# A graph attention layer on one core: softmax tiles turned by DMA instead of by TensorE, score stacks written from PSUM by halves

## The chip, the cores and the metric

The kernel runs on one core of one Trainium2 chip. The metric is device time in microseconds, the median of several executions; lower is better. A core has TensorE (PE, with its weight loads listed as PEld), VectorE (DVE), ScalarE (ACT), GpSimd (POOL), and 16 DMA engines, which are fed mainly from the queue of SyncE (SP). Each engine takes its instructions in the order in which they were written, and waits on semaphores for what other engines make.

## The reference

A layer norm and a relu give h (384 nodes, 1024 features). Three projections of h, and a second projection of each, give q2, k2 and v2 in 16 heads of 64. A mask is built from 6528 edges. Then comes a masked softmax per head, its product with v2, an output projection, and the residual.

```
h = jnp.maximum(_layernorm(x, axis=-1), 0.0)
q = x @ wq.T + bq ; k = x @ wk.T + bk ; v = x @ wv.T + bv          # x here is h
q2 = (q @ wiq.T + biq).reshape(N, H, D).transpose(1, 0, 2)          # k2, v2 alike
scores = jnp.einsum('hnd,hmd->hnm', q2, k2) * scale + mask[None]
attn = jax.nn.softmax(scores, axis=-1)
out = jnp.einsum('hnm,hmd->hnd', attn, v2)
return x + (out.transpose(1, 0, 2).reshape(N, OUT_F) @ wo.T + bo)
```

All is float32 to nearly full precision.

## The kernel before

**Arithmetic.** Each float32 operand is split into a high part (float32r, made by ScalarE in `split_hi`, L71) and a low part, the difference (`split_lo`, L83, on VectorE or GpSimd, at L86). A product is three matmuls: high x high, high x low, low x high (`mm3`, L373). The weights come in chunks of 128 rows (0.5 MB): 8 each for v, q, iv and k, then iq and ik in turn (one pair of chunks makes q2 and k2 of two heads), then 8 for the output. A chunk is loaded five chunks ahead of its use, into four raw buffers, and split two chunks ahead.

**Stages.** From 0 to about 150 us: layer norm, the projections, and beside them the building of the mask by indirect DMA from GpSimd. From about 150 to 285 us: attention. It is a loop over steps (L825), one softmax tile a step; a tile is 128 nodes of one head against all 384, so a head is three tiles, t = 0, 1, 2, and there are 48 tiles.

**A step.** Step i writes, in this order, each to the engine that does it:
- TensorE: half of the step's fill, the score matmuls of tile i (`do_S`), the other half of the fill. The fill is q2/k2 chunks (`fill_qk`), later blocks of the output projection (`fill_o`); about eight matmuls a step.
- VectorE: `do_ttr` of tile i-1 (masked scores and their row minimum, from PSUM into an SBUF tile e); for t = 0 `do_low` of tile i-4.
- ScalarE: `do_exp` of tile i-2 with the row sums.
- VectorE: `do_norm` of tile i-3, the reciprocal of the row sums. For t = 1 and 2 GpSimd then multiplies e by it (L738). For t = 0 ScalarE writes the high plane in fp16 instead (`do_high`), and a step later VectorE the low plane (`do_low`, L748).
- Every third step TensorE turns tiles t = 1 and 2 of a head by three 128x128 transposes each into PSUM (`turn_mm`, L758), alternating with the six matmuls of an earlier head's product with v2 (`av_mm`, L773). ScalarE and VectorE copy the turned tiles to fp16 high and low parts (`do_pt`, L766 and L767). Tile t = 0 is turned by a DMA from SP (`do_turn`, L752).
- ScalarE and VectorE finish a head's product (`do_ao`), and every second head ScalarE and GpSimd split it (`do_aos`).
- Tasks: where a q2/k2 chunk begins, `qk_head` evacuates the chunk before it (`qk_done`), splits the weights two chunks on, and loads the one five on.

**Score stacks.** `qk_done` evacuates a chunk (128 rows, two heads of 64) into a tile nat, high on ScalarE (L384), low on VectorE (L385), and then copies pieces of it by DMA: four for q2, four for k2, so that one head's high and low parts lie above each other in the 128 partitions. The score is then two matmuls: stacked q (high over low) by k high over k high, and by k low over k low.

**Weight splits in the attention stage.** The low parts of the odd chunks are on GpSimd, those of the even ones on VectorE (`PAR`). The output weights are split at the steps in `WSTEPS`, with the low part on GpSimd for 2, 3, 4 and 6 (`OPOOL`).

**Output.** `fill_o` builds six blocks (three node tiles by two halves) over the eight chunks, in two parts of four chunks, with three PSUM banks "g". The sum of a finished first part (`ysum`, L663) frees its bank; `flush_y` writes it.

Of the kernel before, what the change touches and what calls it, by code (L numbers as in the profile page):

```python
# [26 lines left out]
def gnn_kernel(ctx: ExitStack, tc: tile.TileContext, x, edges, erows, etw, wq, wk, wv, wiq, wik, wiv, wo,  # L27
# [355 lines left out]
    def evac(ps, hi, lo, bias):  # L383
        nc.scalar.activation(hi, ps[:, :N], AF.Identity, bias=bias)  # L384
        nc.vector.scalar_tensor_tensor(lo, ps[:, :N], bias, hi.bitcast(F32), op0=OP.add, op1=OP.subtract)  # L385

# [6 lines left out]
    w = 0  # L393
# [125 lines left out]
    def v2_early():  # L519
        t = work.tile([128, 2, N], F32R, tag="nat", name="tv", bufs=2)  # L520
        tv = t.bitcast(F32).rearrange("p a n -> p (a n)")[:, :512]
        nc.scalar.activation(tv, accs[5], AF.Copy)
        accs[5] = tv
# [45 lines left out]
    gps = {}  # L569

    def qk_done(w):
        n, p = chunks[w]
        q2 = nc.scalar if p == 0 else nc.sync
        nat = work.tile([128, 2, N], F32R, tag="nat", name="nat", bufs=2)
        evac(gps[w], nat[:, 0, :], nat[:, 1, :], bc[:, (3 if n == "iq" else 4) * 8 + p:(3 if n == "iq" else 4) * 8 + p + 1])
        nf = nat.bitcast(F32)
        if n == "iq":
            qs = work.tile([128, 2, N], F32R, tag="qs", name="qs")
            qf = qs.bitcast(F32)
            nc.sync.dma_start(qf[0:64, 0, :], nf[0:64, 0, :])  # L580
            q2.dma_start(qf[64:128, 0, :], nf[0:64, 1, :])
            nc.sync.dma_start(qf[0:64, 1, :], nf[64:128, 1, :])
            q2.dma_start(qf[64:128, 1, :], nf[64:128, 0, :])
            stacks["q", p] = qs
        else:
            ks = work.tile([128, 2, 2, N], F32R, tag="ks", name="ks")
            kf = ks.bitcast(F32)
            for o in range(2):
                for r in range(2):
                    (q2 if r else nc.sync).dma_start(kf[r * 64:(r + 1) * 64, o, :, :], nf[o * 64:(o + 1) * 64, :, :])  # L590
            stacks["k", p] = ks
# [7 lines left out]
    def qk_head(w):  # L599
# [5 lines left out]
        split_lo(w + 2, nc.gpsimd if (w + 2) % 2 == PAR else None)  # L605
# [24 lines left out]
    DT = (0,)  # L630
    PRE, RATE, RATE_O, RATE_E = 84, 7.9, 8, 8
    WSTEPS = (37, 40, 42, 44, 47, 51)
    PAR, OPOOL, ODVE = 1, (2, 3, 4, 6), (2,)
# [38 lines left out]
    def fill_o():  # L672


        first = [(0, 0), (0, 1), (1, 0), (1, 1), (2, 0), (2, 1)]
        first += [(a, k) for k in (2, 3) for a in range(3)] + [(a, k) for a in range(3, 6) for k in range(KH)]
        for a, k in first:
            while now[0] < wready[k] or now[0] < 6 * k + OREADY:
                yield 0
            if k == 0:  # L680
                flush_y(1)
# [6 lines left out]
        todo = [(a, k) for k in range(KH, 7) for a in range(5)]  # L688
        while todo:
# [6 lines left out]
            if k == KH:  # L696
                flush_y(1)
# [7 lines left out]
    def do_S(i):  # L705
# [4 lines left out]
        for s in range(2):  # L710
            nc.tensor.matmul(ps[:, :N], qs[:, o, t * 128:(t + 1) * 128], ks[:, o, s, :], start=(s == 0), stop=(s == 1))  # L711

    def do_ttr(i):
        t = i % 3
        e = es[i] = work.tile([128, N], F32, tag="e", name="e", bufs=EB)
        s = sts[i] = work.tile([128, 4], F32, tag="s", name="s", bufs=12)
        nc.vector.tensor_tensor_reduce(e, st_ps.pop(i)[:, :N], ma[:, t, :], -0.125, 3.0e38, OP.add, OP.min, s[:, 0:1])  # L717

    def do_exp(i):
        s = sts[i]  # L720
        nc.scalar.activation(es[i], es[i], AF.Exp, bias=s[:, 0:1], scale=-1.0, accum_out=s[:, 1:2])  # L721
# [3 lines left out]
    def pt_setup():  # L725
# [4 lines left out]
        plv.extend(f[:, 2 * j:2 * j + 2, :] for j in range(3))  # L730

    def do_norm(i):
        s = sts[i]
        nc.vector.reciprocal(s[:, 2:3], s[:, 1:2])  # L734
        if i % 3 in DT:
            nc.vector.tensor_scalar(s[:, 2:3], s[:, 2:3], PSC, None, op0=OP.mult)
        else:
            nc.gpsimd.tensor_tensor(es[i], es[i], s[:, 2:3].to_broadcast([128, N]), OP.mult)  # L738

    planes = {}  # L740

# [172 lines left out]
```

## Time and profile before

| | |
|---|---|
| median of 3 runs | 294.54 us (294.42 to 294.67) |
| profiled execution | 294.56 us, its span 292.8 us |
| TensorE clock granted | 1.0 throughout |
| attention stage | about 150 to 285 us |
| score matmuls of the first and the last tile | 160.1 and 265.1 us |
| DMA moved | 54.6 MB, 187 GB/s over the span |

A line of a group names the kernel line, engine, operation, output and inputs, shape and count, then the busy time and the mean of one. In a timeline the first two columns are the start and the duration in us; a wait ahead of an instruction, with what ended it, stands in brackets. Matmuls are pipelined, so that one starts before the one ahead of it has ended; the cost of one is the distance between starts. PEld is the row of weight loads; its share shows best how dense TensorE's work is.

### The profile page before, as it was taken

The numbers are of one execution on the slowest core, as the hardware profiler recorded it, in microseconds if no ns is written. First come the engines' busy times: TensorE is split into PE (matmuls) and PEld (weight loads), VectorE is DVE, ScalarE is ACT, GpSimd is POOL, SyncE is SP. The second block draws the span as 40 slices with busy tenths as digits, with TensorE's granted clock in tenths as the row PEclk, the third lists the DMA queues.
The fourth block names the chain that finished last, engine by engine and source line by source line (L and its number), as shares of the span: only waits on it lengthen the run. The fifth ranks groups of instructions, "written<-read, shape, count | busy, mean of one in ns | idle before, by whom it ended". The sixth has DMA issues, their size and how long they took to land. (4 is left out here: it accounts for less than half of the span.)

```text
span 292.8 us, 4859 instructions
## 1 busy us (share of the span) xinstructions
PE 284.7 (97%) x1610; PEld 267.4 (91%) x1610; DVE 208.2 (71%) x509; ACT 159.7 (55%) x291; POOL 154.8 (53%) x153
## 2 busy tenths in 40 slices
PE   6999999999999999999999999999999999989995
PEld 5999999999988889999999999999999998868874
DVE  3858996667665452999966768878786876788623
ACT  3894543244331222343643778787878788766510
POOL 3765576437775787992004256262627268636210
PEclk9999999999999999999999999999999999999999
DMA  7799857973463342278438879879797969901105
GB/s 268 248 321 404 292 209 254 323 242 112 143 189 122 121 146 72 72 224 296 154 86 227 241 208 211 212 166 227 166 234 147 254 133 234 230 2 27 27 3 215
DMA packets 33305, 54.60 MB, mean 187 GB/s; under 512 B 17408, under 2 KB 20992, under 8 KB 33280
## 3 DMA queue, kind: packets, MB, share of 16 engines
q1 hardware_dynamic: 30896, 51.90, 61.4%
q0 software_dynamic: 2064, 1.80, 2.2%
q10 hardware_dynamic: 320, 0.59, 0.8%
q8 instruction: 13, 0.21, 0.3%
q14 instruction: 12, 0.10, 0.1%
HBM read 38.30 MB, written 3.39 MB: 142 GB/s over the span
## 5 line engine op out<-in xcount | busy, mean ns | idle before, releaser
L374 PE MATMUL g<-g,whl 128*128 128x384 f32 x312 | 105.8, 339 | 0.0
L376 PE MATMUL g<-g,whl 128*128 128x384 f32 x312 | 104.3, 334 | 0.0
L375 PE MATMUL g<-g,whl 128*128 128x384 f32 x312 | 104.2, 334 | 0.0
L231 POOL DMA_INDIRECT tab<-val,idx x51 | 59.7, 1171 | 32.0 <-issue 11.8
L81 ACT ACTIVATE whl<-raw 128x1024 fp32r<-128x1024 f32 x51 | 53.5, 1050 | 29.8 <-PE g L376 21.1
L86 DVE TENSOR_TENSOR whl<-raw,whl 128x1024 fp32r<-128x1024 f32 x41 | 53.8, 1313 | 20.1 <-ACT whl L81 17.0
L374 PEld LDWEIGHTS g<-g,whl 128*128 128x128 f32 x312 | 58.6, 188 | 0.2
L375 PEld LDWEIGHTS g<-g,whl 128*128 128x128 f32 x312 | 58.6, 188 | 0.0
L376 PEld LDWEIGHTS g<-g,whl 128*128 128x128 f32 x312 | 58.6, 188 | 0.1
L390 ACT ACTIVATE g<-f,bc 128x384 fp32r<-128x384 f32 x24 | 14.8, 618 | 53.7 <-DVE f L389 44.8
L738 POOL TENSOR_TENSOR e<-e,s 128x384 f32<-128x384 f32 x32 | 26.4, 829 | 31.2 <-DVE s L734 23.0
L86 POOL TENSOR_TENSOR whl<-raw,whl 128x1024 fp32r<-128x1024 f32 x11 | 26.3, 2395 | 25.9 <-ACT whl L81 25.0
L721 ACT ACTIVATE e<-e,s 128x384 f32<-128x384 f32 x48 | 29.1, 607 | 2.0 <-DVE s L717 1.2
L717 DVE CUSTOM_DVE_ANT_0 e<-s,ma 128x384 f32<-128x384 f32 x48 | 26.4, 552 | 4.3 <-PE s L711 3.7
L389 DVE TENSOR_TENSOR f<-g,rrow 128x384 f32<-128x384 f32 x24 | 13.3, 554 | 18.0 <-PE g L376 18.0
L773 PE MATMUL a<-pt,vhl 128*128 128x384 f16 x96 | 26.1, 326 | 0.0
L758 PE MATMUL t<-ident,e 128*128 128x128 f32 x96 | 24.9, 272 | 0.0
L711 PE MATMUL s<-ks,qs 128*128 128x384 f32 x96 | 24.5, 335 | 0.0
L767 DVE SCALAR_TENSOR_TENSOR pt<-t,pt 128x384 f16<-128x384 f32 x32 | 16.6, 549 | 8.2 <-ACT pt L766 8.2
L799 POOL TENSOR_TENSOR g<-aof,g 128x384 fp32r<-128x384 f32 x8 | 8.3, 1041 | 25.5 <-ACT g L798 25.5
L711 PEld LDWEIGHTS s<-ks,qs 128*128 128x128 f32 x96 | 17.5, 188 | 0.9
L744 ACT ACTIVATE pt<-e,s 128x384 f16<-128x384 f32 x16 | 9.9, 616 | 15.4 <-issue 9.4
(166 smaller groups left out, 447.0 us busy)
## 6 DMA issues: line engine op xcount, KB each, us to landing
ks<-nat SPq DMA_DIRECT2D x30, 192.0 KB
raw<-in_wv_dram SPq DMA_DIRECT2D x8, 512.0 KB
raw<-in_wq_dram SPq DMA_DIRECT2D x8, 512.0 KB
raw<-in_wiv_dram SPq DMA_DIRECT2D x8, 512.0 KB
raw<-in_wk_dram SPq DMA_DIRECT2D x8, 512.0 KB
raw<-in_wiq_dram SPq DMA_DIRECT2D x8, 512.0 KB
raw<-in_wik_dram SPq DMA_DIRECT2D x8, 512.0 KB
raw<-in_wo_dram SPq DMA_DIRECT2D x8, 512.0 KB
```

The costliest lines, as they stand in the source:

```text
L81: nc.scalar.activation(dst[0], raw[w], AF.Copy)
L86: (eng or nc.vector).tensor_tensor(lo, raw[w], hi.bitcast(F32), OP.subtract)
L231: nc.gpsimd.indirect_dma_start(out=tabs[c // RNG], out_offset=bass.IndirectOffsetOnAxis(ap=idx[:, c:c + 1], axis=0), in_=val[:, c:c + 1], ...
L374: nc.tensor.matmul(ps, lhi, rhi, start=first, stop=False)
L375: nc.tensor.matmul(ps, lhi, rlo, start=False, stop=False)
L376: nc.tensor.matmul(ps, llo, rhi, start=False, stop=last)
L711: nc.tensor.matmul(ps[:, :N], qs[:, o, t * 128:(t + 1) * 128], ks[:, o, s, :], start=(s == 0), stop=(s == 1))
L717: nc.vector.tensor_tensor_reduce(e, st_ps.pop(i)[:, :N], ma[:, t, :], -0.125, 3.0e38, OP.add, OP.min, s[:, 0:1])
L721: nc.scalar.activation(es[i], es[i], AF.Exp, bias=s[:, 0:1], scale=-1.0, accum_out=s[:, 1:2])
L738: nc.gpsimd.tensor_tensor(es[i], es[i], s[:, 2:3].to_broadcast([128, N]), OP.mult)
L758: nc.tensor.transpose(ps[:, k * 128:(k + 1) * 128], es[i][:, k * 128:(k + 1) * 128], ident)
L773: nc.tensor.matmul(ps[:, :N], vhl[:, k, h, :, :], ptv[h % 3][:, 3 * s + k, :], start=(k == 0 and s == 0), stop=(k == 2 and s == 1))
```

## The change

- **Turning.** `DT` becomes (0, 1, 2): all three tiles of a head are turned by DMA, except tiles 1 and 2 of the last head. So 46 tiles of 48 go by DMA and two by TensorE; before, 16 and 32.
- **Planes.** Every tile turned by DMA gets a high and a low plane. The high plane is ScalarE's for t = 0 and GpSimd's for t = 1 and 2 (`PHI`), where it takes the place of the multiplication by the reciprocal; the low plane is VectorE's for all. One reciprocal of three columns, after the head's last tile, serves all three. The planes are made two steps later than before (`LAG`), in five buffers instead of three.
- **Order.** A head's product with v2 comes one step later (3h + 11), but for the last head.
- **Score stacks.** The evacuation writes the stacks directly, by halves of 64 partitions: high to its place, low across to the other half. For k2, a second copy of the high part goes by DMA, two copies a pair; the stacks of k2 lie in two fixed buffers whose other low half is set to zero once.
- **Weight splits.** All low parts in this stage that `qk_head` issues go to GpSimd.
- **Output.** The blocks of the first part come block by block for two chunks at a time; the sums are written at the end of each step; two steps of `WSTEPS` move (37 to 36, 40 to 38).

```
-    def evac(ps, hi, lo, bias):
-        nc.scalar.activation(hi, ps[:, :N], AF.Identity, bias=bias)
-        nc.vector.scalar_tensor_tensor(lo, ps[:, :N], bias, hi.bitcast(F32), op0=OP.add, op1=OP.subtract)
...
+    ksb = []
+    for j in range(2):
+        ksb.append(work.tile([128, 2, 2, N], F32R, tag="ks", name="ks"))
+        for o in range(2):
+            nc.gpsimd.memset(ksb[j].bitcast(F32)[64 - o * 64:128 - o * 64, 1, o, :], 0.0)
...
+        for o in range(2):
+            m, l = slice(o * 64, o * 64 + 64), slice(64 - o * 64, 128 - o * 64)
+            hi, lo = (qs[m, o, :], qs[l, o, :]) if n == "iq" else (ks[m, 0, o, :], ks[m, 1, o, :])
+            nc.scalar.activation(hi, ps[m, :N], AF.Identity, bias=bias[m])
+            if n == "ik":
+                kf = ks.bitcast(F32)
+                (nc.scalar if p == 0 and o else nc.sync).dma_start(kf[l, 0, o, :], kf[m, 0, o, :])
+            nc.vector.scalar_tensor_tensor(lo, ps[m, :N], bias[m], hi.bitcast(F32), op0=OP.add, op1=OP.subtract)
...
-        split_lo(w + 2, nc.gpsimd if (w + 2) % 2 == PAR else None)
+        split_lo(w + 2, nc.gpsimd)
...
-    DT = (0,)
+    DT, LAG, PHI = (0, 1, 2), 2, (1, 2)
-    WSTEPS = (37, 40, 42, 44, 47, 51)
-    PAR, OPOOL, ODVE = 1, (2, 3, 4, 6), (2,)
+    WSTEPS = (36, 38, 42, 44, 47, 51)
+    OPOOL, ODVE = (2, 3, 4, 6), (2,)
...
-        first = [(0, 0), (0, 1), (1, 0), (1, 1), (2, 0), (2, 1)]
-        first += [(a, k) for k in (2, 3) for a in range(3)] + [(a, k) for a in range(3, 6) for k in range(KH)]
+        first = [(a, k) for c in (0, 2) for a in range(3) for k in (c, c + 1)]
+        first += [(a, k) for a in range(3, 6) for k in range(KH)]
...
-        todo = [(a, k) for k in range(KH, 7) for a in range(5)]
+        todo = [(a, k) for k in range(KH, 7) for a in (0, 1, 3, 4, 2)]
...
+    def by_dma(i):
+        return i % 3 in (DT if i < S - 3 else (0,))
...
+        last = max(c for c in range(3) if by_dma(3 * h + c))
+        if by_dma(i) and t < last:
+            return
+        c = slice(0, t + 1) if by_dma(i) else slice(t, t + 1)
+        nc.vector.reciprocal(s[:, 2, c], s[:, 1, c])
...
+        planes[i] = plv[next(npl) % len(plv)]
+        if i % 3 in PHI:
+            nc.gpsimd.tensor_tensor(planes[i][:, 0, :], es[i], factor(i).to_broadcast([128, N]), OP.mult)
+        else:
+            nc.scalar.activation(planes[i][:, 0, :], es[i], AF.Copy, scale=factor(i))
...
-        a_at[3 * h + 10 if h < 15 else 3 * h + 9] = h
+            if not by_dma(3 * h + t):
+                t_at.setdefault(3 * h + 7 if h < 15 else 3 * h + 5 + t, []).append(3 * h + t)
+        a_at[3 * h + 11 if h < 15 else 3 * h + 9] = h
...
-        if 0 <= i - 4 < S and (i - 4) % 3 in DT:
+        if 0 <= i - 4 - LAG < S - 3 and by_dma(i - 4 - LAG):
+            do_low(i - 4 - LAG)
+        if i - 4 == S - 3:
             do_low(i - 4)
...
+        for j in [i - 3 - LAG] if i - 3 - LAG < S - 3 else []:
+            if j >= 0 and by_dma(j):
+                do_high(j)
...
+        flush_y()
```

## The prediction

> **What bounds the kernel now.** I read the page's shares first, then a table by stage, then TensorE's instructions in order, then groups by tile, then VectorE and GpSimd side by side.
>
> From the page, and from the table by stage (columns: stretch, its length, busy PE, PEld, DVE, ACT, POOL, clock, DMA share, GB/s):
> ```profile
> PE 284.7 (97%) x1610; PEld 267.4 (91%) x1610; DVE 208.2 (71%) x509; ACT 159.7 (55%) x291; POOL 154.8 (53%) x153
> ...
> 170.00:240.00 70.00, 70.00 (x430) 68.06 (x430) 53.89 (x159) 56.36 (x126) 34.12 (x31) 1.00 0.85 194
> ```
> TensorE has no gap in the attention stage: 70 of 70 us, weight loads 97%. VectorE has 77%, ScalarE 81%, GpSimd 49%. TensorE's order sets the pace.
>
> TensorE in order of time, then a piece of the chain that ended last:
> ```profile
> 200.14 0.27 PE L758 MATMUL t<-ident,e 128*128 128x128 f32 x1
> 200.25 0.33 PE L773 MATMUL a<-pt,vhl 128*128 128x384 f16 x1
> 200.41 0.27 PE L758 MATMUL t<-ident,e 128*128 128x128 f32 x1
> ...
> 260.25 0.50 PE L374 MATMUL g<-whl,g 128*128 128x512 f32 x1 [1.37 <-DVE res L663]
> ```
> ```profile
> 279.27 0.99 PE a L773 x6
> ```
> A busy time overlaps the next one; starts give the price. Turn and product together take 0.27 us; six products alone take 0.99, 0.165 each. So a turn costs TensorE 0.107, not the 0.272 of its row. The last line of the first fence is the stage's one stall, 1.4 us for a bank that an output sum holds.
>
> The group by tile of the planes (min/median/max), and VectorE and GpSimd in order of time:
> ```profile
> L748 DVE SCALAR_TENSOR_TENSOR pt<-e,s,pt x16: 611/619/1754, 166.6 to 267.9; 128x384 f16<-128x384 f32 x16
> L752 SPq DMA_TRANSPOSE pt<-pt x16: 1212/1234/1825, 172.5 to 269.7; - x16
> ```
> ```profile
> 219.74 0.56 ACT L384 ACTIVATE nat<-g,bc 128x384 fp32r<-128x384 f32 x1
> 220.21 1.05 ACT L81 ACTIVATE whl<-raw 128x1024 fp32r<-128x1024 f32 x1
> 220.31 0.83 POOL L738 TENSOR_TENSOR e<-e,s 128x384 f32<-128x384 f32 x1
> 220.34 0.62 DVE L385 SCALAR_TENSOR_TENSOR nat<-g,bc,nat 128x384 fp32r<-128x384 f32 x1 [0.79 <-ACT nat L384]
> 220.87 0.55 DVE L717 CUSTOM_DVE_ANT_0 e<-s,ma 128x384 f32<-128x384 f32 x1
> 221.33 2.39 POOL L86 TENSOR_TENSOR whl<-raw,whl 128x1024 fp32r<-128x1024 f32 x1 [0.20 <-ACT whl L81]
> 221.34 0.16 DVE L734 RECIPROCAL s<-s 128x1 f32<-128x1 f32 x1
> ...
> 266.82 2.40 POOL L86 TENSOR_TENSOR g<-raw,g 128x1024 fp32r<-128x1024 f32 x1 [2.08 <-ACT g L81]
> 267.88 1.75 DVE L748 SCALAR_TENSOR_TENSOR pt<-e,s,pt 128x384 f16<-128x384 f32 x1 [0.24 <-ACT pt L744]
> ```
> The reader is to see the one long low plane. It began 1.06 us into a GpSimd subtraction, waited for its end at 269.22 and ended 0.41 us later: 1.13 us lost. The evacuation at 220.34, with PSUM as one source, ran 0.62 us beside GpSimd and lost nothing. The splits at 121.57 and 130.06, which read two SBUF tiles on VectorE, took 2.43 and 2.37 us instead of 1.23 beside GpSimd's residual sum.
>
> **What leaves TensorE.** 30 tiles x 3 turns x 0.107 = 9.6 us. A head takes 6.86 us now (the groups of products end at 180.29 and, nine heads on, 242.07); without six turns 6.22. Output sums at the end of each step, and the new order of blocks, put the sum of the first block two steps ahead of its bank's next use: the 1.4 us stall goes (bounds 0 and 1.5).
>
> **What the other engines gain, a head.** A start-to-start cost is below the duration; I take 0.50 for the mask-and-minimum, 0.53 for a low plane, the head's sum and a half evacuation.
> - VectorE: 5.29 (53.89 over 10.2 heads), less two low parts from PSUM (0.549 each), two reciprocals (0.156; for the joint one the 128x3 row of 0.17) and half a weight split (1.226), plus two low planes (0.62) and a second half evacuation (0.62): about 5.1.
> - ScalarE: 5.5 less two copies (0.482) plus one half evacuation (0.574; by the 64-partition row 0.669): 5.1.
> - GpSimd: 3.3 plus half a split (2.39): 4.5. The high planes replace the norms at 0.829; fp16 output has no GpSimd row, so bounds 0.83 and the 1.04 of the ao split; I take 0.83, the same form.
> - SP: three transposes (1.23, worst 1.83), a load and one copy (about 0.6 each): 4.9 of 6.22.
> - DMA: a transpose kept the 16 engines busy for about 1.0 us (271.0 to 272.0, 197 KB). Two more a head add 2 us; the pair's copies fall from 1.18 MB to 0.2 MB, which at that rate takes away 2.5 a head. Neutral.
> - The four memsets of the zero halves (0.41 each by the 128x384 row) lie at 140 to 150 us, where GpSimd is idle.
> - One step more before a head's product costs TensorE nothing while the turns land. A transpose lands 2.2 us after its issue begins (269.71 to 271.9); with a 0.5 MB load (1.5, at the 350 GB/s of the fastest half microseconds) and a copy ahead about 4.5, of three steps, 6.2. Bounds 0 and 1 us a head; I take 0.
>
> All fits under 6.22 by load. What doesn't fit is the order.
>
> **The wait that is added.** A low plane reads two SBUF tiles; there are now three a head, one in every step, and every weight split is on GpSimd, where 2.39 us is longer than any pause between low planes. Follow a step that opens a chunk of q2/k2 (steps 1, 4, ..., 34). On ScalarE: half, half, split high. On VectorE behind them: half, half, mask-and-minimum, low plane. In the fence above that race stands without the second half, which delays both alike: from the evacuation's start GpSimd's subtraction began after 1.59 us, and VectorE's instruction in the low plane's place after 1.60. The subtraction also had to be first only just: at 130.06 GpSimd had started 0.02 us before VectorE and VectorE waited it out. Where it loses, the low plane waits 2.4 us; behind it stand the head's reciprocals, behind those ScalarE's high plane of tile 0, and behind that, in ScalarE's order, the next chunk's evacuation and split. That closes a loop:
> - subtraction 2.39; low plane's rest, reciprocal and factor to ScalarE 0.75 (0.41 after the subtraction; 224.34 to 224.76, less the 0.08 by which the reciprocal starts early);
> - ScalarE: high 0.52, exp 0.60, head's bias 0.69, exp 0.60, ao 0.41 every second head, two halves 0.47 each;
> - split high 1.05 and the hop 0.07.
>
> Sum 7.8 us a head, over TensorE's 6.22 and over the 6.86 of now. Where the low plane wins, the head runs at 6.22, but tile 0's plane then meets what is left of the subtraction (about 1.2 us), VectorE falls behind and the next race is lost by over 0.6: two heads in 14.0, 7.0 each. With two races in three lost I take 7.4. Ten splits (steps 7 to 34) meet low planes: 10 x (7.4 - 6.22) = 11.8 us. GpSimd's four output-weight splits (steps 36, 38, 42, 47) meet low planes too, but VectorE has no evacuations then (1.06 a head): 0 to 1 us each; 1.5 in all.
>
> [...]
>
> [...]
>
> **Sum.** The profiled execution took 294.56 (span 292.8), the median is 294.54: no correction. 294.56 - 9.6 - 1.4 + 11.8 + 1.5 = 296.9, say 297. Its own range: all heads at 7.0 and no later cost, 291; all at 7.8 and 4 later, 303.
>
> **The rivals.**
> - *TensorE stays the bound* (the other side). Place: the low plane behind a chunk's evacuation. The subtraction falls into time that VectorE and ScalarE have to spare (18% by load) and no loop forms. For it: loads of 5.1, 5.1 and 4.5 against 6.22, and 15 of 16 low planes undisturbed today. Against it: today one step in three has a low plane, and it stands ahead of the split. 294.56 - 11.0 + 1.5 = 285. It decides at a delay of (294.56 - 285)/10 = 0.96 us a head: below it the change is faster.
> - *The transposes are late.* SP or the 16 DMA engines hold each head's product up. For it: SP at 79%, issues of up to 1.83 us when the DMA is full (share 0.85 now). Against: DMA load unchanged, some 1.7 us of slack. At 1.2 us for 14 heads: 283.6 + 16.8 = 300; it decides at 0.79.
> - *The turns cost nothing on TensorE*, hidden beside products. Excluded by the starts above.
>
> **How the numbers follow.** Loop 0.52 (slower 0.45, same 0.03, faster 0.04: its low end lies just under the time of now); TensorE bound or a little above it, 283 to 291, 0.38, all faster; late transposes 0.08, slower; the rest, 0.02, no change. Faster 0.42, same 0.05, slower 0.53 (0.2%, 0.6 us, is about what a measurement here can tell). The range 285 to 303 leaves out some 0.12 below, the better end of the bound TensorE, and 0.07 above.
>
> **What would show it.** Right: low planes with a median near 0.6 and every third or so over 1.5 us, ending 0.4 after a GpSimd subtraction; ScalarE's high plane waiting for VectorE's factor; heads 7 to 7.8 us apart; weight loads well under 97%; TensorE waiting for VectorE in the score tiles. Wrong: heads 6.2 to 6.4 apart and weight loads still at 97% (first rival), or TensorE waiting for DMA at the head's product (second). The forecast falls if GpSimd's subtraction regularly starts after the low plane, or if the low plane's wait lies in VectorE's spare time.

## The result, and the profile after

The changed kernel takes 331.88 us (median of 4 runs, 330.38 to 332.09), the kernel before beside it 294.61 (294.42 to 295.71). The ratio is 1.1246, with a 95% interval of 1.1203 to 1.1288: 37 us slower. The profiled execution took 332.09, its span is 330.4.

The page of the kernel after, and its table by stage (columns as before: stretch, length, busy PE, PEld, DVE, ACT, POOL, clock, DMA share, GB/s):

```profile
PE 290.1 (88%) x1520; PEld 256.8 (78%) x1520; DVE 234.5 (71%) x487; ACT 159.6 (48%) x277; POOL 181.5 (55%) x165
```
```profile
170.00:270.00 100.00, 73.10 (x365) 60.40 (x363) 78.83 (x146) 57.07 (x118) 51.35 (x36) 0.97 0.55 121
...
180.00:190.00 10.00, 7.74 (x33) 6.62 (x33) 6.25 (x11) 3.90 (x10) 4.07 (x3) 0.83 0.90 184
```

TensorE was busy 70 of 70 us before (170 to 240 us) and is now busy 73 of 100 (170 to 270 us). No engine has taken its place: VectorE, the busiest, has 79%, and part of that is waiting inside its instructions: its 30 low planes in this stretch take 22.5 us more than at 0.61 us each, its 11 scalings of the factors 2.0 more than at 0.17. What is lost is lost in waits. The view of waits between 150 and 330 us (who waited, for whom, us in total, times, longest) names three engines in a ring:

```profile
PE s L704 <- DVE s L712: 30.0, 30, 2.2
ACT pt L757 <- DVE s L745: 20.0, 8, 2.7
...
ACT pl L757 <- DVE s L745: 15.2, 6, 3.4
...
ACT ks L582 <- DVE ks L586: 9.2, 8, 3.6
ACT qs L582 <- PE s L704: 8.5, 6, 2.8
```

ScalarE waits 35.2 us for the joint factor of a head's three tiles (L745). TensorE waits 30 us for VectorE to free a score bank (L712). ScalarE also waits for VectorE between the halves of a chunk (L586 before the second L582). Here is one head, from one GpSimd subtraction (L86) to the next, in order of time:

```profile
209.50 2.39 POOL L86 TENSOR_TENSOR whl<-raw,whl 128x1024 fp32r<-128x1024 f32 x1 [2.29 <-ACT whl L81]
...
209.51 2.79 DVE L761 SCALAR_TENSOR_TENSOR pt<-e,s,pt 128x384 f16<-128x384 f32 x1
...
212.23 0.17 DVE L743 RECIPROCAL s<-s 128x3 f32<-128x3 f32 x1
212.43 0.17 DVE L745 TENSOR_SCALAR s<-s 128x3 f32<-128x3 f32 x1
...
212.63 0.61 ACT L757 ACTIVATE pt<-e,s 128x384 f16<-128x384 f32 x1 [2.61 <-DVE s L745]
...
213.15 0.60 ACT L717 ACTIVATE e<-e,s 128x384 f32<-128x384 f32 x1
...
213.87 0.67 ACT L806 ACTIVATE aot<-a,bc,vsc 64x384 f32<-64x384 f32 x1
...
214.57 0.61 ACT L717 ACTIVATE e<-e,s 128x384 f32<-128x384 f32 x1
...
215.31 0.58 ACT L582 ACTIVATE ks<-g,bc 64x384 fp32r<-64x384 f32 x1
...
216.12 0.60 DVE L586 SCALAR_TENSOR_TENSOR ks<-g,bc,ks 64x384 fp32r<-64x384 f32 x1
...
216.76 0.58 ACT L582 ACTIVATE ks<-g,bc 64x384 fp32r<-64x384 f32 x1 [0.88 <-DVE ks L586]
...
217.36 1.06 ACT L81 ACTIVATE whl<-raw 128x1024 fp32r<-128x1024 f32 x1
...
218.49 2.39 POOL L86 TENSOR_TENSOR whl<-raw,whl 128x1024 fp32r<-128x1024 f32 x1 [3.83 <-ACT whl L81]
```

GpSimd started 0.01 us ahead of the low plane, and the low plane (L761) took 2.79 us instead of 0.61: it ended only after the subtraction had. Such a wait of a VectorE instruction for a GpSimd one, or the other way round, inside its own time, is called a wait at the port below; the word is a name only, since the traces show the wait and not what the two engines share. Behind the low plane stand the reciprocal and the factor, behind the factor ScalarE's high plane (it had waited 2.61), and behind that, in ScalarE's order, exponential, bias, exponential, two halves and the next weight split, which starts the next subtraction. Such low planes of 2.77 to 2.84 us start at 179.78, 190.50, 199.53 and so on to 266.46, ten in ten heads. A head that closes with a k2 chunk takes 8.99 us (209.50 to 218.49), one with a q2 chunk 9.98 (199.52 to 209.50); before it was 6.86.

From the score matmul of tile 0 to that of tile 36, before takes 77.4 us (160.28 to 237.63) and after 106.2 (160.42 to 266.60), 28.8 more. From tile 36 to 47, it is 27.5 and 33.7, 6.2 more. That is 35.0 of the 37.3 us.

### The profile page after: what moved, and what is told of

Read it like the earlier page. It is cut to its first block, busy times and chain, and to the rows that moved or that the text cites. A ratio compares the mean times of both kernels' runs of the same rounds, so it can differ in the third digit from the quotient of the medians.

```text
span 330.4 us, 4621 instructions
## 1 busy us (share of the span) xinstructions
PE 290.1 (88%) x1520; PEld 256.8 (78%) x1520; DVE 234.5 (71%) x487; ACT 159.6 (48%) x277; POOL 181.5 (55%) x165
## 4 chain that ended last, share of the span: by engine, by line
PE 54%; DVE 25%; ACT 8%; issue 7%; POOL 2%; DMA 2%; SPq 0%; DVEq 0%; ACTq 0%; POOLq 0%
PE g L376 13%; PE g L374 13%; PE g L375 13%; DVE pt L761 7%; DVE e L712 6%; DVE pl L761 4%; DVE qs L586 2%; ACT aot L806 2%; ACT qs L582 2%; DMA g<-in_x_dram 2%; DVE ks L586 2%; PE s L704 2%; ACT e L717 2%; PE s L374 2%; PE s L376 2%
## 5 line engine op out<-in xcount | busy, mean ns | idle before, releaser
L374 PE MATMUL g<-g,whl 128*128 128x384 f32 x312 | 107.0, 343 | 0.0
L376 PE MATMUL g<-g,whl 128*128 128x384 f32 x312 | 105.6, 338 | 0.0
L375 PE MATMUL g<-g,whl 128*128 128x384 f32 x312 | 105.5, 338 | 0.0
L86 POOL TENSOR_TENSOR whl<-raw,whl 128x1024 fp32r<-128x1024 f32 x19 | 47.4, 2497 | 62.7 <-ACT whl L81 54.7
L704 PE MATMUL s<-ks,qs 128*128 128x384 f32 x96 | 28.8, 382 | 32.8 <-DVE s L712 30.0
L86 DVE TENSOR_TENSOR whl<-raw,whl 128x1024 fp32r<-128x1024 f32 x33 | 44.1, 1336 | 15.3 <-ACT whl L81 15.3
L761 DVE SCALAR_TENSOR_TENSOR pt<-e,s,pt 128x384 f16<-128x384 f32 x28 | 35.0, 1249 | 2.8 <-ACT pt L757 1.6
L712 DVE CUSTOM_DVE_ANT_0 e<-s,ma 128x384 f32<-128x384 f32 x48 | 26.4, 552 | 2.6 <-PE s L704 1.5
L761 DVE SCALAR_TENSOR_TENSOR pl<-e,s,pl 128x384 f16<-128x384 f32 x18 | 20.5, 1141 | 2.7 <-POOL pl L755 1.6
L755 POOL TENSOR_TENSOR pt<-e,s 128x384 f16<-128x384 f32 x19 | 17.7, 944 | 7.3 <-POOL whl L86 5.0
L586 DVE SCALAR_TENSOR_TENSOR qs<-g,bc,qs 64x384 fp32r<-64x384 f32 x16 | 9.9, 616 | 16.3 <-ACT qs L582 16.3
L807 DVE SCALAR_TENSOR_TENSOR aof<-a,vsc,aot 64x384 f32<-64x384 f32 x16 | 9.9, 616 | 12.7 <-ACT aot L806 12.7
L786 PE MATMUL a<-pt,vhl 128*128 128x384 f16 x96 | 18.4, 327 | 0.1
```

What stands on the lines that cost most here:

```text
L86: (eng or nc.vector).tensor_tensor(lo, raw[w], hi.bitcast(F32), OP.subtract)
L374: nc.tensor.matmul(ps, lhi, rhi, start=first, stop=False)
L375: nc.tensor.matmul(ps, lhi, rlo, start=False, stop=False)
L376: nc.tensor.matmul(ps, llo, rhi, start=False, stop=last)
L586: nc.vector.scalar_tensor_tensor(lo, ps[m, :N], bias[m], hi.bitcast(F32), op0=OP.add, op1=OP.subtract)
L761: nc.vector.scalar_tensor_tensor(pl[:, 1, :], es.pop(i), factor(i), pl[:, 0, :], op0=OP.mult, op1=OP.subtract)
```

## The experiments

**One link of the ring at a time.** The reading above gives a theory (called theory 1 at first, and once it had been widened theory A): an order of instructions that closes on itself through ScalarE, VectorE and GpSimd. The first four kernels each loosen one link. They keep all of the work.

*The low part of every q2/k2 weight split on VectorE.*

```diff
-        split_lo(w + 2, nc.gpsimd)
+        split_lo(w + 2)
```

> One edit to the changed kernel: the low parts of the weight splits of the q2/k2 chunks go to VectorE (1.23 us each) instead of GpSimd (2.39 us). Theory 1 (the loop through the port pair: a low plane waits for the whole subtraction, the reciprocals behind it, ScalarE behind those): no low plane near 2.8 us is left in the chunk steps, heads fall from 9.6 us to 6.6 to 7.5, the time to 300 to 308. Theory 2 (the evacuation by halves, with ScalarE's second half waiting for VectorE's first, is what slows the heads, and the long low planes lie in time that is lost anyway): VectorE only gets more work, the time stays at 325 to 340. Theory 3 (transposes come late): unchanged, about 332.

Measured: 331.01 us, 1.1221 (1.1133 to 1.1308). Theory 1's 300 to 308 is missed; the time is inside the 325 to 340 of theory 2 (the halves are the main cause) and at the 332 of theory 3 (late transposes). The mean of the low planes fell to 0.67 us in one of their two groups and 0.80 in the other, so the wait at the port was gone from the chunk steps, but the reciprocals still stood 8.52 apart (213.64 to 222.16): VectorE's own subtraction, 1.23 us and 0.46 of waiting, lay in the same place of the ring, and ScalarE still waited about 2.1 us a head for the factor. So it is not this wait as such that costs. Something stands between two factors whichever engine subtracts.

*Both high halves ahead of both low halves in `qk_done`.* In the change ScalarE's second half waits while VectorE does the first low half.

```diff
             nc.scalar.activation(hi, ps[m, :N], AF.Identity, bias=bias[m])
...
+        for o in range(2):
+            m, l = slice(o * 64, o * 64 + 64), slice(64 - o * 64, 128 - o * 64)
...
             nc.vector.scalar_tensor_tensor(lo, ps[m, :N], bias[m], hi.bitcast(F32), op0=OP.add, op1=OP.subtract)
```

> One edit to the changed kernel: the evacuation writes both high halves first and both low halves after them, so that ScalarE's second half need not stand behind VectorE's first. Theory 1: the loop gets shorter by that wait, 0.8 to 0.9 us a head over some 11 heads, 9 us in all: about 323; the long low planes stay at 2.8 us. Theory 2 (the halves are the main cause): most of the loss goes, below 305. If the wait between the halves is not due to the order of writing, nothing changes: 332.

Measured: 322.91 us, 1.0946 (1.0853 to 1.1039), so 9.0 us less, as theory 1 had it; theory 2, below 305, is missed. The wait between the halves is on the path.

*The weight split ahead of the chunk's evacuation in `qk_head`.*

```diff
+        split_hi(w + 2)
+        split_lo(w + 2, nc.gpsimd)
+        load(w + 5)
         if pendq:
             pendq.pop(0)()
...
-        split_hi(w + 2)
-        split_lo(w + 2, nc.gpsimd)
-        load(w + 5)
```

> One edit to the changed kernel: where a chunk begins, the weight split of the chunk two ahead is issued before the evacuation of the chunk just done, not after it. All the work is the same. Theory 1: GpSimd's subtraction starts some 2 us earlier against the low plane and is nearly over when that arrives; the low planes behind it take 0.6 to 1.3 us, the loop opens, heads 6.3 to 7.3 us, time 292 to 305. Theory 2: the halves still wait for each other, time above 322. Theory 3: unchanged, about 332.

Measured: 312.2 us, 1.0583 (1.0467 to 1.0699), 19.7 us less. In the chunk steps all low planes but one (1.01 us) took 0.6 to 0.7 us, and heads were 7.6 to 7.9 apart from 186 us on. What now stands behind the split are the low halves from PSUM, 0.61 and 0.62 us each here. In the kernel with all three links loosened, below, two of them took 1.25 us together from 213.31, inside a subtraction from 212.50 to 214.86, so there they lost nothing beside it. Beside the splits of the output weights two low planes still took 2.73 and 2.32 us. The time is above the 305 that theory 1 expected at most, and below the 322 and 332 of the others: between 150 and 300 us ScalarE still waited 22.9 us for factors (12.6 and 10.3; 33.6 in the changed kernel), although in the chunk steps the low planes ahead of the reciprocal no longer waited at the port.

*GpSimd's subtraction in two pieces of 512 columns.*

```diff
-        split_lo(w + 2, nc.gpsimd)
+        for c in (slice(0, 512), slice(512, D)):
+            if w + 2 < NCH:
+                nc.gpsimd.tensor_tensor(whl[w + 2][1][:, c], raw[w + 2][:, c], whl[w + 2][0].bitcast(F32)[:, c], OP.subtract)
```

> One edit to the changed kernel: GpSimd's subtraction of a q2/k2 chunk in two instructions of 512 columns instead of one of 1024. Theory 1: a low plane that loses the race waits for 1.2 us instead of 2.4 and gets the ports between the two; the longest low planes are about 1.6 us, the loop is shorter by 1.1 us a head over some 11 heads: about 319. Where GpSimd keeps the ports from one instruction to the next, the low planes stay at 2.8 us. Theory 2 and 3: unchanged, about 332.

Measured: 327.71 us, 1.1109 (1.1025 to 1.1192), 4.2 us less and not the 13 expected. The timeline of this kernel shows who took the rest:

```profile
215.59 2.84 POOL L602 TENSOR_TENSOR whl<-raw,whl 128x512 fp32r<-128x512 f32 x2 [3.84 <-ACT whl L81]
...
215.60 1.69 DVE L763 SCALAR_TENSOR_TENSOR pl<-e,s,pl 128x384 f16<-128x384 f32 x1
...
217.21 0.17 DVE L745 RECIPROCAL s<-s 128x3 f32<-128x3 f32 x1
...
217.41 1.04 DVE L747 TENSOR_SCALAR s<-s 128x3 f32<-128x3 f32 x1
```

The low plane got in between the two pieces and saved 1.1 us. Then the scaling of three factors per partition, 0.17 us elsewhere, waited 0.87 us for the second piece and ended as that ended (218.43). The factor reached ScalarE hardly sooner. The reciprocal just ahead, of the same 128x3 tile, ran its 0.17 us undisturbed.

**The factor's place, and the parts of the change apart.** Theory A now puts the cost in the order: the reciprocal stands behind a low plane on VectorE, and ScalarE's whole stream stands behind the reciprocal.

*The joint factor one step earlier.*

```diff
+        if 0 <= i - 2 < S - 3 and (i - 2) % 3 == 2:
+            do_norm(i - 2)
-        if 0 <= i - 3 < S:
+        if 0 <= i - 3 < S and not (i - 3 < S - 3 and (i - 3) % 3 == 2):
             do_norm(i - 3)
```

> The changed kernel, with the joint reciprocal of a head (and its scaling) issued one step earlier, right behind the head's last exponential, ahead of the chunk's evacuation and of the low planes on VectorE's queue. All the work stays. Theory A (an in-order loop between ScalarE and VectorE: the reciprocal stands behind the low plane of the head before on VectorE, and ScalarE's first high plane, with every exponential and evacuation half behind it, stands behind the reciprocal): the 35.2 us that ScalarE waits for the factors between 150 and 330 us fall below 8 us and the time falls by 22 to 36 us, to 296 to 310. Theory B (the wait of the low plane behind GpSimd's weight subtraction costs its length, 2.2 us a head, wherever the reciprocal stands): the time stays within 6 us of the changed kernel, 326 to 335.

Measured: 323.9 us, 1.0991 (1.0928 to 1.1055), 8 us less. Neither theory had this. ScalarE's wait for factors between 150 and 300 us fell from 33.6 to 2.5 us, as theory A said, and the time did not follow. VectorE was now busy 88 of 100 us: between 207 and 224 us its low planes still took 2.82 and 2.80 us behind the subtraction, and the scaling and another low plane 0.79 and 1.26 behind the rest of it and GpSimd's high planes. ScalarE now waited for VectorE elsewhere, at the halves (20.7 us; 14.6 in the changed kernel). A link that opens leaves the others closed.

*This, the split first and the high halves first, together:* the three diffs shown for them, in one kernel.

> The earlier reciprocal, with the weight split issued ahead of the chunk's evacuation and both high halves of a chunk ahead of both low halves. All the work stays. Theory A (the loop between ScalarE and VectorE): with its three links open the head comes near to TensorE's own 6.2 to 6.6 us, 284 to 296 us. Theory B (the port alone): the split ahead of the evacuation had already taken the port wait away and reached 312 us, the halves in order are worth 9 us at most, so 303 to 312.

Measured: 306.62 us, 1.0405 (1.0351 to 1.0459). The three gains alone add up to 36.7 us; together they are 25.3, and 12 us remain above the kernel before. Theory A's 284 to 296 is missed, so the loop is not the whole of it. The time lies in the 303 to 312 of theory B (the port alone), against which the run with the splits on VectorE speaks: no wait at the port in the chunk steps, and 331.0 us. In this kernel's table by stage and its timeline:

```profile
210.00:220.00 10.00, 9.44 (x54) 8.49 (x53) 9.10 (x20) 8.72 (x18) 7.08 (x5) 1.00 0.75 161
...
230.00:240.00 10.00, 9.05 (x50) 8.00 (x51) 9.73 (x19) 7.50 (x16) 5.47 (x5) 1.00 0.89 153
```
```profile
218.50 2.46 POOL L86 TENSOR_TENSOR whl<-raw,whl 128x1024 fp32r<-128x1024 f32 x1 [1.75 <-ACT whl L81]
...
218.65 0.16 DVE L746 RECIPROCAL s<-s 128x3 f32<-128x3 f32 x1
...
218.85 2.14 DVE L748 TENSOR_SCALAR s<-s 128x3 f32<-128x3 f32 x1
```

VectorE is busy 91% and 97% of these stretches, and there is a new victim at the port: the scaling of 384 numbers took 2.14 us. It is not this head's alone. Between 170 and 270 us the 13 scalings take 14.2 us more than at 0.17 us each and the 39 low planes 10.0 more than at 0.61: 24 us together, as much as the 24.5 of the changed kernel in the same stretch, though over some 13 heads instead of 10. With the split first the low planes of the chunk steps had been free of that wait; with the factor early as well, the scaling meets the subtraction in their place. So this kernel does not show what the change would cost without these waits.

*The halves undone, the turning kept:* `qk_done`, staging tile and DMAs of before, with one staging tile instead of two (there was no room for two).

```diff
-            nc.scalar.activation(hi, ps[m, :N], AF.Identity, bias=bias[m])
...
-            nc.vector.scalar_tensor_tensor(lo, ps[m, :N], bias[m], hi.bitcast(F32), op0=OP.add, op1=OP.subtract)
+        nat = work.tile([128, 2, N], F32R, tag="nat", name="nat", bufs=1)
...
+            nc.sync.dma_start(qf[0:64, 0, :], nf[0:64, 0, :])
...
```

> The changed kernel, with the score stacks of q2 and k2 as before: one full evacuation in two instructions into a staging tile, and DMAs into the stacks; one staging tile instead of two, for room. Turning, high planes, lags and the output's order stay changed. Theory A: the wait of ScalarE's second half for VectorE's first low half (0.8 to 1.0 us a head over 16 chunks) and 0.3 us of overhead of the second half go, the factor's loop stays: 312 to 320 us. If the halves alone were what costs: 297 or less. If the turning alone costs and the halves are worth what they were said to save, about the changed kernel's 332.

*The turning undone, the halves kept.*

```diff
-    DT, LAG, PHI = (0, 1, 2), 2, (1, 2)
+    DT, LAG, PHI = (0,), 2, (1, 2)
```

> The changed kernel, with tiles 1 and 2 of each head turned on TensorE again, as before; tile 0's planes still two steps later, halves, all low splits on GpSimd and the output's order stay changed. Theory A: ScalarE no longer waits for a joint factor behind three tiles, but the halves still hold it for 0.8 us a head and tile 0's low plane may still meet GpSimd's subtraction: 298 to 312 us. If the turning is not what costs (the halves or the splits are): 320 or more. If the turning is all that costs: 293 to 297.

Measured: 318.18 us, 1.0797 (1.0728 to 1.0867), for the turning without the halves, and 314.06, 1.0658 (1.0597 to 1.0719), for the halves without the turning. Against 294.7 for the kernel before in these runs, the turning without the halves costs 23.5 us and the halves without the turning 19.4. Both together cost 37 and not 43. Each part makes the kernel slower without the other. Neither figure is the clean price of one part: both kernels keep all low parts of the splits on GpSimd and the new order of the output, the first has one staging tile fewer than before, and the second makes the planes of tile 0 two steps later. The first came out as theory A had it (312 to 320). The 312 expected at most without the turning was too low; the halves were dearer than thought.

*The halves without the turning, with high halves first and split first:* the diff just shown, with the two of the first group.

> Tiles 1 and 2 of a head turned on TensorE as before, with the score stacks written by halves, but both high halves ahead of both low halves and the weight split ahead of them. All the work stays. If the 19.5 us that the changed kernel without the turning stood above the kernel before are the price of the halves in their written order (1.2 us a chunk over 16 chunks): 295 to 303 us. If the halves cost nothing and the splits on GpSimd do: 308 or more.

Measured: 302.81 us, 1.028 (1.025 to 1.031), at the upper end of the 295 to 303 expected. So 11 of the 19.4 us were the halves' and the split's place in the order. The other 8 or so stay; ScalarE is busy 83 of 100 us there. Which part of them is the second instruction of each half, and which the splits all on GpSimd, was not taken apart.

**Looking for the bound of what is left.** Two more on top of the kernel with all three links loosened.

```diff
-        ps = st_ps[i] = bank("s")
+        ps = st_ps[i] = bank("ts"[i % 2])
```

> The kernel with the earlier factors, the weight split first and the high halves first, in which the scores of alternate tiles use the two PSUM banks that the turned tiles left, so four banks in place of two. All the work stays. There TensorE waited 11.2 us for the reduction on VectorE to free a score bank, and ScalarE and VectorE then waited for the chunk that stands behind those scores on TensorE. If the loop closes through TensorE's order (theory A, with TensorE in it): 290 to 300 us. If VectorE's own queue, 92 us busy of 100 with its waits for the port, is the bound: 303 to 308 us.

Measured: 305.78 us, 1.0381 (1.0343 to 1.0418), 0.8 below the kernel without it, which is hardly more than the scatter of two runs each (305.34 to 306.22 and 305.97 to 307.26). TensorE's wait for a score bank was thus a follower, as the second branch had it. That branch names VectorE's queue, 93 us busy of 100, as the bound; the run does not show this by itself, and some 24 of the 93 us are again waiting in scalings and low planes.

*The four banks, and the subtraction in four pieces of 256 columns.*

```diff
-        split_lo(w + 2, nc.gpsimd)
+        for c in range(0, D, D // 4):
+            if w + 2 < NCH:
+                c = slice(c, c + D // 4)
+                nc.gpsimd.tensor_tensor(whl[w + 2][1][:, c], raw[w + 2][:, c], whl[w + 2][0].bitcast(F32)[:, c], OP.subtract)
```

> The same with four score banks, and GpSimd's subtraction of the weights in four instructions of 256 columns in place of one of 1024. With the port handed over between instructions, no operation of VectorE waits over 0.8 us for it, where the scaling of 128x3 factors took 2.14 us and low planes 2.4 to 2.8 us: 3 to 10 us below the kernel with four banks. If every piece holds the next operation up, so that the waits only spread: within 3 us of it.

Measured: 302.74 us, 1.0277 (1.0248 to 1.0307): 3.0 less, on the line between the two branches (3 to 10, and within 3). VectorE is still busy 89 of 100 us; the waiting in scalings and low planes fell from some 24 to some 17 us, all of it in the scalings. The cut is in the q2/k2 splits alone: beside the uncut splits of the output weights low planes still took 2.75 and 2.80 us.

**The third part alone.** The kernel before with the new order of the output's blocks, the new steps of the output weights and the sums right behind each step.

```diff
-    WSTEPS = (37, 40, 42, 44, 47, 51)
+    WSTEPS = (36, 38, 42, 44, 47, 51)
...
-        first = [(0, 0), (0, 1), (1, 0), (1, 1), (2, 0), (2, 1)]
-        first += [(a, k) for k in (2, 3) for a in range(3)] + [(a, k) for a in range(3, 6) for k in range(KH)]
+        first = [(a, k) for c in (0, 2) for a in range(3) for k in (c, c + 1)]
+        first += [(a, k) for a in range(3, 6) for k in range(KH)]
...
-        todo = [(a, k) for k in range(KH, 7) for a in range(5)]
+        todo = [(a, k) for k in range(KH, 7) for a in (0, 1, 3, 4, 2)]
...
+        flush_y()
```

> The kernel before with the third part of the change alone: the order of the output's blocks, the steps of the output weights, and the sums right behind each step. If the 1.4 us in which TensorE stood for a bank of the output is freed: 292.8 to 293.8 us. If another wait takes its place: 294.2 to 295.5 us.

> The output's order alone once more, for its interval: 292.8 to 293.8 us if the one bank wait freed is worth 1.1 us, 294.2 to 295.5 if not.

Measured: 293.4 us, 0.9958 (0.9902 to 1.0014), and with 12 runs 293.26, 0.9945 (0.9923 to 0.9968). TensorE's wait of 1.37 us for a bank at 260.25 is gone, and the time is 1.4 us lower (293.26 against 294.66 beside it). This is the one version that beats the kernel before, by half a per cent.

**Can the turning be had otherwise?** In the frame of before, with a factor for each tile, a step behind its exponential, tile 1 and then also tile 2 of each head but the last went to the DMA. The edit goes on top of the new output order; with three tiles, `DT` is (0, 1, 2).

```diff
-    DT = (0,)
+    DT = (0, 1)
...
-        planes[i] = plv[i // 3 % 3]
+        planes[i] = plv[next(npl) % len(plv)]
```

> The kernel before, with the third part of the change (the output's order) and tile 1 of each head but the last turned by DMA as well as tile 0. Score stacks, alternating weight splits, lags and separate factors stay as before. All the work stays. If the transposes on TensorE are what the time hangs on and the loop of the changed kernel comes from its joint factor and its halves: 15 tiles by 0.32 us are 4.8 us below the order alone, 287.5 to 290.5 us. If the turning itself costs (two low planes a head that may wait at the port, stacks and transposes on one busy DMA path): 293 to 300 us.

> The same with all three tiles of each head but the last turned by DMA, so the whole turning of the change in the frame of before: a tile's factor on its own right after its exponential, its high plane on ScalarE one step later and its low plane one step after that, stacks by DMA. All the work stays. If the joint factor, the lag and the halves made the changed kernel's loop: TensorE stays the bound or nearly, 284 to 291 us. If the transposes by DMA cannot keep up beside the stacks' DMAs, whose share of the time was 0.87 already, or the port holds three low planes a head: 296 to 318 us.

Measured: 329.73 us, 1.1175 (1.1134 to 1.1216), with two, and 356.39, 1.2065 (1.202 to 1.2111), with three. Both are far beyond what either branch had. In the waits between 170 and 270 us of the kernel with three, ScalarE's high plane waited 22.6 us for a transpose that still read its buffer, of which there were three for three tiles a head, and 18.5 us under the name "issue"; the granted clock of TensorE was 0.81 there. So these two runs mix two causes, and the next one gave the planes two more buffers, taken from the exponentials.

```diff
-    EB = 6
+    EB = 4
...
+        f = work.tile([128, 4, N], F16, tag="pl", name="pl", bufs=1)
+        plv.extend(f[:, 2 * j:2 * j + 2, :] for j in range(2))
```

> All three tiles turned by DMA in the frame of before, now with five planes in place of three, for which the exponentials' buffers go from six to four. With three planes ScalarE waited 41 us of 100 (22.6 named DMA, 18.5 named issue) for a plane that a transpose still read. If the planes are what held it: 300 to 325 us. If the exponentials' buffers or SP's queue, on which a transpose stands behind the stacks' DMAs, hold it as long: 340 us or more.

Measured: 337.1 us, 1.1452 (1.1367 to 1.1538), between its two branches. No wait for a transpose is left in that stretch, and yet a head takes about 10 us. In order of time:

```profile
220.03 0.61 DVE L752 SCALAR_TENSOR_TENSOR pt<-e,s,pt 128x384 f16<-128x384 f32 x1
...
220.56 0.15 DVE L737 RECIPROCAL s<-s 128x1 f32<-128x1 f32 x1
...
220.75 0.15 DVE L739 TENSOR_SCALAR s<-s 128x1 f32<-128x1 f32 x1
...
220.99 0.62 ACT L748 ACTIVATE pt<-e,s 128x384 f16<-128x384 f32 x1 [2.02 <-issue]
```

The high plane that stood 2.02 us under "issue" starts 0.09 us after the scaling of its factor ends; it is the factor that it waited for. The row sums of its tile had been there since 215.81. In between VectorE had an evacuation's low part and a weight subtraction, both of which waited for ScalarE, then a mask-and-minimum and the low plane of the tile before, all ahead of the reciprocal. That is the same kind of ring as in the change, but from 191 us on two of a head's three tiles meet it (waits of 2.0 to 2.9 and of 1.3 to 1.4 us) instead of one wait a head. Whether the two fewer buffers of the exponentials cost anything was not taken apart. In the kernel before, tiles 1 and 2 are multiplied by their factor on GpSimd, so ScalarE's stream meets such a wait once a head.

*The turning with the old stacks, its factor early and its split first; then also with four banks and four pieces:* the diffs shown above for each, in one kernel.

> The changed kernel with the score stacks of before (one evacuation, DMAs), the joint factor of a head one step earlier and the weight split ahead of the evacuation. All the work stays. If the turning costs only by its joint factor (36 us of ScalarE's waits for it between 150 and 300 us without the halves): 292 to 304 us. If transposes and stacks on one busy DMA path are the bound (share 0.97 without the halves): 308 to 318 us.

> The same with four score banks and GpSimd's subtraction in four pieces: with the halves in place these were worth 3.9 us together. 2 to 6 us below it; within 1 us of it if the port no longer stands on the path that sets the end.

Measured: 316.71 us, 1.076 (1.0714 to 1.0806), and 319.85, 1.0867 (1.0724 to 1.1009). ScalarE's waits for factors were no longer among the larger ones, and the first of the two came out as its second branch had it. The second missed: it was to be 2 to 6 us below the first, or within 1, and is 3.1 above. TensorE waits longer for transposes there (15.4 against 10.9 us in the largest row of weight loads); why, was not followed up. In the view of waits (170 to 270 us) of the first kernel:

```profile
ACT nat L384 <- DMA ks<-nat: 16.9, 6, 3.5
PEld L791 <- DMA pt<-pt: 10.9, 5, 3.3
...
ACT nat L384 <- DMA qs<-nat: 8.2, 5, 2.3
```

ScalarE's evacuation waits 25 us for the stacks' copies to leave the one staging tile, and TensorE waits for transposes; the DMA share is 0.97. With a second staging tile, part of this might go; there was no room to try it. With the turning, and as long as the old stacks have one staging tile, the halves cost 13.7 us more than the old stacks in the change's order (331.9 against 318.2), and 10.1 less with the factor early and the split first in both and the high halves first (306.6 against 316.7). So against old stacks with one staging tile it was the order of the halves that cost, not the writing by halves itself.

## Why the prediction was wrong

The forecast was 297.0 us, 285 to 303, with slower at 0.53. It came out slower, at 331.9. The way and the mechanism were right, the size was not: ten heads took 9.63 us and not 7.4, which is 22 of the 35 us that the forecast is short. Point by point, by its own steps:

- *TensorE is the bound before, and leaves it.* Right. What it was freed from was not had by anybody: it waited for score banks instead.
- *The output's order is worth 1.4 us.* Right: 1.4 us measured by itself.
- *The loads fit under 6.22 us a head.* Near. Over 100 us with 10.4 heads of 9.63, ScalarE has 5.5 us a head (5.1 said), GpSimd 4.9 (4.5) and VectorE 7.6, of which ten waits of about 2.2 us are 2.1, so 5.5 (5.1). That the sums fit said nothing about the time.
- *Late transposes.* Right to set aside for the change itself: no wait for a transpose is among its large waits. With the old stacks they came.
- *The loop, closed by a low plane that waits for the subtraction.* The mechanism was right, with its place, its price (2.2 us in ten low planes) and the order behind it. Its size was not. The sum let nothing but the low planes wait for GpSimd, and no run shows that: in the changed kernel a scaling of factors (172.65) took 2.21 us beside a subtraction from 172.45 to 174.83, while the low halves from PSUM lost nothing beside one (213.31, with all three links loosened). Two terms failed.
  - "Two races in three lost". Ten of ten were lost. The recorded starts lie 0.01 to 0.02 us apart in nine, GpSimd ahead; in the tenth the low plane's (190.50) is 0.04 us ahead of the subtraction's (190.54) and it took 2.84 us all the same, so at this distance the recorded order does not name the winner. The race was called a tie from rows of the kernel before, and it isn't one that is drawn anew: the ring brings both engines to the same point in each head, VectorE from the same half evacuation as ScalarE. That is the step from 7.4 to 7.8, 4 us over ten heads. (By the prediction's own figures two losses in three make 7.3 and not 7.4.)
  - "Two halves 0.47 each". The head of 7.8 us was a sum of ScalarE's instructions back to back. In the k2 head above, 8.99 against 7.61 without the ao term: 0.98 is the wait of the second half for VectorE's first low half, 0.13 the half's length of 0.60, 0.26 the two exponentials at 0.72 and 0.74 with the reading of their sums, 0.01 the rest. In the q2 head before it, 9.98 against 8.02 with the ao term, it is 0.79 between the halves, and 0.75 in which ScalarE waits for TensorE to finish the chunk, which itself is late for want of a score bank. The wait between the halves is written in the diff: the low half is issued inside the loop, behind the high one. The prediction put two halves on each engine and no order between them. The run with the high halves first took 9.0 us off.
- *1.5 us for the output weights.* From tile 36 to 47 the change loses 6.2 us against before, where the steps of the prediction gave a gain. Low planes of 2.74 and 2.32 us stand at 273.11 and 290.28, and TensorE's clock fell there too (0.86 from 280 to 290 us). No run took this stretch apart, so the cause of this part stays open.
- *The rival that decides at 0.96 us a head* was lost by far: from 9.63 to 6.22 is 3.4.

What the prediction did not see is that the loop has no single cover. It priced one wait and took the ring of 6.22 for granted behind it. With the port's wait moved off (312.2), with the factor early (323.9), and with all three (306.6), the ring stays above before. Without the turning, the halves alone are above before by 19.4. By the code and the traces, the change puts the one factor that ScalarE's in-order stream waits for on VectorE right behind a chunk's halves and a low plane; in the kernel before, no low plane stands in the step of tile 0's reciprocal. What stays open is the price of the parts of the last 8 to 12 us. With the three links loosened VectorE is busy for 92 us of 100, so its queue is likely the bound; that is read from its share and from the small effect of more banks, and no run took work off VectorE to show it. Some 24 of these 92 us are still waiting in scalings and low planes, so the wait at the port is a rival that these runs do not exclude; cutting the subtractions in four took away some 7 us of that waiting and 3.0 us of the time.

## What to carry to other kernels

Loads that fit under the new bound say nothing until the order has been walked: write down for each in-order engine which instruction waits for which other engine, follow it until it comes back to where it began, and add that ring up with every hand-over in it. A pair of instructions that alternates between two engines makes each wait for the other: here ScalarE's second half cost it 0.98 and 0.79 us in the two heads above, and VectorE waited 0.64 and 0.65 us for it. Where a ring has several links, one link opened shows a part or nothing, and gains of single links do not add up; an experiment that opens them all is what tells whether the idea can pay, and its own trace has to be read before it is taken as such: here one wait had only gone over to another instruction.

## What the runs showed of the hardware

**A tiny operation waits at the port too.** The scaling of a 128x3 tile on VectorE takes 0.17 us alone, 1.04 beside a 512-column subtraction of GpSimd (217.41, in the kernel with two pieces) and 2.14 beside one of 1024 (218.85, with all three links loosened), ending within 0.03 us of it. The reciprocal of the same tile ran its 0.16 to 0.17 us beside both. Why the one waits and the other does not, the traces do not show. The prediction's sum had only low planes pay.

**VectorE gets in between two pieces.** With the subtraction in two pieces the low plane that came 0.01 us late (215.60) took 1.69 us and not 2.79, and ran before the second piece was done; the two pieces together took 2.84 us and not 2.39.

**GpSimd loses as well.** In the changed kernel its second high plane of a head, where VectorE's low plane was ahead (183.53 against 183.71), took 1.14 us instead of 0.83.

**TensorE's clock fell after some short pauses.** In the changed kernel, in order of time on TensorE:

```profile
183.37 0.73 PE L704 MATMUL s<-ks,qs 128*128 128x384 f32 x2 [1.76 <-DVE s L712]
183.90 0.52 PE L374 MATMUL g<-g,whl 128*128 128x384 f32 x1
184.22 0.52 PE L375 MATMUL g<-g,whl 128*128 128x384 f32 x1
...
187.30 0.34 PE L374 MATMUL g<-g,whl 128*128 128x384 f32 x1
187.47 0.34 PE L375 MATMUL g<-g,whl 128*128 128x384 f32 x1
```

After a pause of 1.76 us the products stood 0.32 us apart instead of 0.17, for 3.4 us (183.90 to 187.30), and the granted clock of these 10 us is 0.83. The products were slow again from 252.13 to 255.55, behind a pause of 1.78 that ended at 251.09, and from 279.58 to 282.75, behind one of 2.05 (278.30); the granted clock was 0.83 from 250 to 260 us and 0.86 from 280 to 290. Behind pauses of 1.77 (270.05) and 2.17 (297.88) they were not, so the length of the one pause does not decide. Before the change the clock was 1.0 throughout. What lowers the clock, the traces do not show. In the run with the splits on VectorE the granted clock was 0.91 over 100 us (170 to 270). It is not what makes the change slow: its four runs had a mean clock of 0.985 to 1.0, and those at 1.0 took 330.4 and 331.9 us.
